# The last block's tail of a gated attention kernel: three groups' sums and half the projection taken out of it, transfers and store on two queues

## The chip, the cores and the metric

The kernel runs on one core of one Trainium2 chip. The time is the device time of one execution in microseconds (us), the median of several. One further execution was taken with the hardware profiler; the profile and the trace come from it. The engines are called PE (TensorE, matrix products; PEld is its weight load), DVE (VectorE), ACT (ScalarE), POOL (GpSimd) and SP (SyncE, which here only issues transfers). SP and ACT each have a queue on which they issue DMA transfers.

## The reference

The input x has the shape 4 x 2048 x 256, in float32. A layer norm gives xn. One branch is causal attention with 16 heads of 16 columns, rotary positions and an output projection; the other is a feed-forward net with ternary weights and a SiLU behind it, which gates the first:

```python
x = L0_attn_x
xn = _layernorm(x, axis=-1)
s = attention(xn)          # softmax(q k^T / 4, causal) v, then @ Wo.T + bo
g = _silu(ffn(xn))         # ternary W1, gelu, ternary W2
x = x + s * g
```

What matters here is the end of the attention: for each query the weighted sum of the values is divided by the sum of the softmax's exponentials, multiplied by Wo, has bo added, is multiplied by the gate and added to x.

## The kernel before, in words

The 8192 rows are worked off in 16 blocks (`NBLK`) of 512 queries (`NB`), four blocks (`NQ`) for each of the four sequences. A block's 16 heads go in four groups (`G`) of four heads. A loop over the 64 pairs of block and group (from line 1017) runs, for each group, the steps of `values`: scores (L771), exponentials (L778 on ACT), the causal mask on the diagonal (L782 on POOL) and the product with the values (L795), summed up in one PSUM bank `av`. Each head has 32 rows of `av`: 16 of the weighted values, one of the sum of exponentials. Beside them the loop hands out other work: the maxima of the next group (`maxima`, L685 to L745, with its reductions on DVE), the projections of a later block, its feed-forward net, and, one at each step, the entries of a list `deferred`. The order in which things are written is the order on each engine; nothing reorders them afterwards, so an instruction that waits holds up what stands behind it on its engine.

When a group is through, `end` (L820) runs in the first step of the following group, or behind the loop for the very last one. It copies `av` to `av_sb` (L824, ACT) and issues, head by head, two transfers on SP: `y` (L831), 16 rows of 512 values, to the rows of the head in the tile `ys[blk]`, and `w` (L836), the 512 sums laid out as 8 rows of 64 in the tile `ws[blk]`, so that a block's 16 heads fill 128 rows of 64. Head d of the block lies in half `kc` = d // 8 of `y`: two halves of 128 rows.

Behind a block's fourth group `end` puts the steps of `finish(blk)` (L847) on `deferred`:

- `loaded` (L853): x of the block is loaded again, 512 KB, on SP.
- `inverted` (L857, L858): DVE takes the reciprocal of the 128 x 64 sums, and SP writes them to DRAM (`rd`).
- `spread` (L866): SP reads them back in two transfers of 256 KB (`rw`), each head's row of 512 repeated for its 16 rows.
- `divided(kc)` (L876): DVE multiplies `y` by `rw`, one half at a time.
- `projected(dc)` (L886, L893): two products with Wo, one for each `kc`, summed up in a bank; in the profile each is two instructions. DVE adds bo and multiplies by the gate, which gives `s`.
- `added(t2)` (L909, L915): four transposes of `s` on PE, and DVE adds x. Behind the second of them SP stores the block's 512 KB (L924).

In all blocks but the last these steps lie beside the groups of the next block. In the last block nothing follows: behind the loop (L1071 to L1075) the last `end` and then the whole of `finish` run alone.

Of the kernel before, what the change touches and what calls it, by code (L numbers as in the profile page):

```python
# [9 lines left out]
F32 = mybir.dt.float32  # L10
# [4 lines left out]
ALU = mybir.AluOpType  # L15
# [4 lines left out]
P = 128  # L20
NB = 512
TT = NB // P
H = 16
HD = 16
HF = HD // 2
G = 4
GH = H // G
# [11 lines left out]
def attention_gated_by_ffn(  # L39
# [33 lines left out]
    nc = tc.nc  # L73
    B, T, D = x.shape
    FF = w1.shape[0]
    KC = D // P
    FC = FF // P
    NQ = T // NB
    NBLK = B * NQ
# [5 lines left out]
    out_blk = out.rearrange("b (n t p) d -> (b n) p t d", t=TT, p=P)  # L85
# [12 lines left out]
    def bank(name):  # L98
        i = free_banks.pop(0)
        taken.setdefault(name, []).append([i])  # L100
        return psum[:, i, :]
# [30 lines left out]
    woT = const.tile([P, KC, D], F32, name="woT")  # L132
# [619 lines left out]
    def values(blk, g):  # L752

        n = blk % NQ
        mT, q = mTs.pop((blk, g)), qst[blk, g]
        last = (n + 1) * TT - 1
        pending, exs = [], {}

        def scores(kb, j, q0):
            s2 = two_banks("s2")  # L760
            w = NB - q0

            at = NB - 2 * P if kb == last else 0
            if not at:
                exs[j] = pp.tile([P, 2, NB], F32, tag="e", name="e")
            e = exs[j][:, :, at : at + w]
            for part in range(2):
                for a in range(2):
                    rows = slice(a * ST, (a + 1) * ST)
                    k = kst[blk, g, kb // TT][rows, j, (kb % TT) * P : (kb % TT + 1) * P]  # L770
                    nc.tensor.matmul(  # L771
                        s2[:, a, :w],
                        (k, sels[j][rows, :])[part],
                        (q[rows, j, q0:], mT[rows, q0:])[part],
                        start=(part == 0),
                        stop=(part == 1),
                    )
            nc.scalar.activation(e, s2[:, :, :w], AF.Exp, scale=1.0 / math.sqrt(HD))  # L778
            release("s2")
            if kb >= n * TT:  # L780

                nc.gpsimd.affine_select(  # L782
                    out=e[:, :, :P],
                    in_=e[:, :, :P],
                    pattern=[[0, 2], [1, P]],
                    compare_op=ALU.is_ge,
                    fill=0.0,
                    base=0,
                    channel_multiplier=-1,
                )  # L790
            return e

        def times_v(kb, ex, q0):
            for h in range(GH):
                nc.tensor.matmul(  # L795
                    av[h * HP : (h + 1) * HP, q0:],
                    vst[blk, g, kb // TT][:, kb % TT, h * VE : h * VE + HP],
                    ex[h // 2][:, h % 2, : NB - q0],
                    start=(kb == 0),
                    stop=(kb == last),  # L800
                )
            if kb % TT == TT - 1:
                vst.pop((blk, g, kb // TT))
                loads.release("v")

        for kb in range(last + 1):
            q0 = max(kb - n * TT, 0) * P
            ex = [scores(kb, j, q0) for j in range(GH // 2)]
            if kb % TT == TT - 1:
                kst.pop((blk, g, kb // TT))  # L810
                loads.release("k")
            yield
            if kb < last:
                while pending:
                    times_v(*pending.pop())
            pending.append((kb, ex, q0))
            yield
        qst.pop((blk, g))

        def end():  # L820
            for chunk in pending:
                times_v(*chunk)
            av_sb = one.tile([P, NB], F32, tag="av_sb", name="av_sb")
            nc.scalar.copy(av_sb, av)  # L824
            if g == 0:
                ys[blk] = yp.tile([P, KC, NB], F32, tag="y", name="y")
                ws[blk] = small.tile([P, H * NB // P], F32, tag="w", name="w")

            for h in range(GH):
                d = (g * GH + h) * HD  # L830
                nc.sync.dma_start(  # L831
                    out=ys[blk][d % P : d % P + HD, d // P, :],
                    in_=av_sb[h * HP : h * HP + HD, :],
                )
                a = (g * GH + h) * P // H
                nc.sync.dma_start(  # L836
                    out=ws[blk][a : a + P // H, :],
                    in_=av_sb[h * HP + HD : h * HP + HD + 1, :].rearrange(
                        "o (a k) -> o a k", a=P // H
                    ),  # L840
                )
            if g == G - 1:
                deferred.extend(finish(blk))

        ends.append(end)

    def finish(blk):  # L847

        got = {}

        def loaded():
            got["x"] = one.tile([P, TT, D], F32, tag="xr", name="x_res")
            nc.sync.dma_start(out=got["x"], in_=x_blk[blk])  # L853

        def inverted():
            w = ws.pop(blk)
            nc.vector.reciprocal(w, w)  # L857
            nc.sync.dma_start(  # L858
                out=rd[blk].rearrange("h (a k) -> (h a) k", k=H * NB // P), in_=w
            )  # L860

        def spread():

            r = got["r"] = one.tile([P, KC, NB], F32, tag="rw", name="rw")
            for kc in range(KC):
                nc.sync.dma_start(  # L866
                    out=r[:, kc, :],
                    in_=rd[blk][kc * (P // HD) : (kc + 1) * (P // HD)]
                    .unsqueeze(1)
                    .to_broadcast([P // HD, HD, NB]),  # L870
                )

        def divided(kc):
            if kc == 0:
                got["yT"] = tp.tile([P, KC, NB], F32, tag="tT", name="yT")
            nc.vector.tensor_tensor(  # L876
                got["yT"][:, kc, :], ys[blk][:, kc, :], got["r"][:, kc, :], ALU.mult
            )

        def projected(dc):  # L880
            if dc == 0:
                ys.pop(blk)
                got["s"] = tp.tile([P, KC, NB], F32, tag="tT", name="s")
            po = bank("po")
            for kc in range(KC):
                nc.tensor.matmul(  # L886
                    po,
                    woT[:, kc, dc * P : (dc + 1) * P],
                    got["yT"][:, kc, :],
                    start=(kc == 0),  # L890
                    stop=(kc == KC - 1),
                )
            nc.vector.scalar_tensor_tensor(  # L893
                got["s"][:, dc, :],
                po,
                boc[:, dc : dc + 1],
                gs[blk][:, dc, :],
                ALU.add,
                ALU.mult,
            )  # L900
            release("po")

        def added(t2):
            x_sb, s = got["x"], got["s"]
            pt = bank("pt")
            for j in range(2):
                t = 2 * t2 + j
                for dc in range(KC):
                    nc.tensor.transpose(  # L909
                        pt[:, (2 * j + dc) * P : (2 * j + dc + 1) * P],  # L910
                        s[:, dc, t * P : (t + 1) * P],
                        ident,
                    )
            ts2 = slice(2 * t2, 2 * t2 + 2)
            nc.vector.tensor_tensor(  # L915
                x_sb[:, ts2, :],
                pt.rearrange("p (t d) -> p t d", t=2),
                x_sb[:, ts2, :],
                ALU.add,
            )  # L920
            release("pt")
            if t2 == TT // 2 - 1:
                gs.pop(blk)
                nc.sync.dma_start(out=out_blk[blk], in_=x_sb)  # L924

        if (blk + 1) % NQ == 0:

            steps = [None, loaded, None, None, inverted, None, spread, None, None]
            steps += [lambda: [divided(kc) for kc in range(KC)]]
        else:  # L930
            steps = [None, loaded, None, None, inverted, None, spread, None]
            steps += [lambda kc=kc: divided(kc) for kc in range(KC)]
        steps += [lambda dc=dc: projected(dc) for dc in range(KC)]
        steps += [None]
        steps += [lambda t2=t2: added(t2) for t2 in range(TT // 2)]
        return steps

# [1 line left out]

    deferred, ends = [], []

    class Paced:

# [10 lines left out]
        def rest(self):  # L956
            for _ in self.gen:
                pass
# [172 lines left out]
```

## Time and profile before

| | us |
|---|---|
| median of three runs (lowest, highest) | 2438.69 (2438.4, 2438.8) |
| the profiled execution, its own time | 2433.26 |
| its span, from the first to the last instruction | 2431.5 |
| PE busy in the span | 2303.4 |
| DVE, ACT, POOL busy | 1624.9, 1467.2, 893.9 |
| start of the last group's copy (L824) | 2404.04 |
| issue of the last store (L924) | 2427.67 |

The mean granted TensorE clock was 0.985 of full speed. Times inside the profile count from the start of the span. Between the span and the execution's own time lie 1.8 us. Where the text speaks of the landing of a transfer, it is the time from its issue to the last arrival at its semaphore, from the records of the single transfers in the trace. These are the main ones of the last block:

| transfer | size | issue | to landing, us |
|---|---|---|---|
| last `w` (L836) | 2 KB | 2409.40 | 1.71 |
| `rd` (L858) | 32 KB | 2411.97 | 2.35 |
| first `rw` (L866) | 256 KB | 2414.33 | 3.79 |
| second `rw` (L866) | 256 KB | 2415.00 | 4.69 |
| store (L924) | 512 KB | 2427.67 | 2.92 |

### The profile page before, as it was taken

The numbers are of one execution on the slowest core, as the hardware profiler recorded it, in microseconds if no ns is written. First come the engines' busy times: TensorE is split into PE (matmuls) and PEld (weight loads), VectorE is DVE, ScalarE is ACT, GpSimd is POOL, SyncE is SP. The second block draws the span as 40 slices with busy tenths as digits, with TensorE's granted clock in tenths as the row PEclk, the third lists the DMA queues.
The fourth block names the chain that finished last, engine by engine and source line by source line (L and its number), as shares of the span: only waits on it lengthen the run. The fifth ranks groups of instructions, "written<-read, shape, count | busy, mean of one in ns | idle before, by whom it ended". The sixth has DMA issues, their size and how long they took to land.

```text
span 2431.5 us, 43963 instructions
## 1 busy us (share of the span) xinstructions
PE 2303.4 (95%) x16852; PEld 1228.4 (51%) x16852; DVE 1624.9 (67%) x2923; ACT 1467.2 (60%) x1871; POOL 893.9 (37%) x1312
## 2 busy tenths in 40 slices
PE   6799999999999999999999999999999999999996
PEld 4454545545455455544545455454554545455442
DVE  8656677775556676696636668768663666777880
ACT  3454656656765565765766465565676646566664
POOL 2136343235443535315344542522625453531010
PEclk8899999999999999999999999999999999999998
DMA  7344334234253524224234443413524452432311
GB/s 222 110 134 152 98 118 154 65 103 134 79 167 103 180 86 158 76 89 148 63 125 124 149 140 111 151 55 89 169 61 136 125 189 77 132 120 72 86 35 32
DMA packets 247907, 280.59 MB, mean 115 GB/s; under 512 B 108816, under 2 KB 144016, under 8 KB 247696
## 3 DMA queue, kind: packets, MB, share of 16 engines
q1 hardware_dynamic: 244368, 272.54, 35.5%
q10 hardware_dynamic: 3328, 5.24, 0.6%
q8 instruction: 132, 2.16, 0.4%
q14 instruction: 79, 0.65, 0.1%
HBM read 181.08 MB, written 87.52 MB: 110 GB/s over the span
## 4 chain that ended last, share of the span: by engine, by line
PE 73%; DVE 10%; POOL 6%; ACT 6%; issue 3%; DMA 1%; SPq 0%; ACTq 0%; DVEq 0%; POOLq 0%
PE psum L771 19%; PE psum L795 19%; PE psum L685 14%; PE psum L581 5%; PE psum L494 4%; PE psum L562 4%; DVE mx L707 3%; DVE mx L711 3%; PE psum L697 3%; PE psum L520 2%; PE psum L886 2%; ACT e L778 2%; ACT mT L745 1%; POOL qklo L378 1%; ACT g L589 1%
## 5 line engine op out<-in xcount | busy, mean ns | idle before, releaser
L707 DVE TENSOR_REDUCE mx<-psum 128x1 f32<-128x512 f32 (+1 forms) x2048 | 1261.7, 667 | 504.5 <-PE psum L685 348.5
L778 ACT ACTIVATE e<-psum 128x1024 f32<-128x1024 f32 (+3 forms) x1280 | 1081.0, 894 | 646.9 <-PE psum L771 611.5
L685 PE MATMUL psum<-kst,qst 64*128 64x512 f32 (+3 forms) x2560 | 618.9, 423 | 18.8 <-ACT e L778 5.5
L795 PE MATMUL psum<-e,vg 128*32 128x512 f32 (+3 forms) x5120 | 595.0, 541 | 17.3 <-POOL e L782 17.1
L782 POOL TENSOR_SCALAR_AFFINE_SELECT e<-e 128x256 f32<-128x256 f32 x512 | 205.7, 411 | 1010.1 <-ACT e L778 980.4
L771 PE MATMUL psum<-qst,kst 64*128 64x512 f32 (+3 forms) x2560 | 553.5, 395 | 21.0 <-DVE mx L707 5.7
L685 PEld LDWEIGHTS psum<-kst,qst 64*128 64x128 f32 x2560 | 311.3, 185 | 449.8 <-DVE mx L707 284.5
L771 PE MATMUL psum<-mT,sel 64*128 64x512 f32 (+3 forms) x2560 | 515.8, 371 | 6.0 <-ACT mT L745 2.9
L771 PEld LDWEIGHTS psum<-qst,kst 64*128 64x128 f32 x2560 | 283.2, 186 | 171.9 <-ACT e L778 54.9
L771 PEld LDWEIGHTS psum<-mT,sel 64*128 64x128 f32 x2560 | 272.2, 186 | 43.3 <-ACT mT L745 23.2
L575 POOL TENSOR_TENSOR hl<-h,hh 128x512 fp32r<-128x512 f32 x128 | 165.3, 1298 | 155.6 <-ACT h L573 121.5
L795 PEld LDWEIGHTS psum<-e,vg 128*32 128x32 f32 x5120 | 110.0, 108 | 176.3 <-issue 123.1
L711 DVE TENSOR_REDUCE mx<-psum 128x3 f32<-128x384 f32 x256 | 130.3, 552 | 73.8 <-PE psum L697 73.8
L697 PE MATMUL psum<-parts 64*128 64x128 bf16 (+1 forms) x1536 | 151.3, 242 | 0.0
L573 ACT ACTIVATE hh<-psum,b1c 128x512 fp32r<-128x512 f32 x128 | 88.1, 688 | 85.4 <-PE psum L562 85.2
L494 PE MATMUL psum<-xf,wqkvT 128*128 128x512 f32 x256 | 127.8, 624 | 0.4 <-ACT xf L439 0.4
L562 PE MATMUL psum<-xh,w1T 128*128 128x512 f32 x256 | 107.8, 421 | 0.7 <-POOL xh L377 0.5
L581 PE MATMUL psum<-hh,w2T 128*128 128x512 f32 x256 | 107.7, 421 | 0.2 <-ACT w2T L348 0.2
L562 PE MATMUL psum<-xl,w1T 128*128 128x512 f32 x256 | 103.2, 403 | 1.1 <-POOL xl L378 1.1
L581 PE MATMUL psum<-hl,w2T 128*128 128x512 f32 x256 | 103.1, 403 | 0.8 <-POOL hl L575 0.2
L502 ACT ACTIVATE qk<-psum,bqk 128x512 f32<-128x512 f32 x64 | 43.9, 688 | 86.7 <-PE psum L494 85.8
L573 ACT ACTIVATE h<-psum,b1c 128x512 f32<-128x512 f32 x128 | 87.3, 682 | 0.0
(128 smaller groups left out, 1643.2 us busy)
## 6 DMA issues: line engine op xcount, KB each, us to landing
kst<-kd SPq DMA_DIRECT2D x160, 512.0 KB
qst<-qd SPq DMA_DIRECT2D x64, 512.0 KB
vg<-vd SPq DMA_DIRECT2D x160, 166.0 KB
qd<-qkhi SPq DMA_DIRECT2D x32, 512.0 KB
qd<-qklo SPq DMA_DIRECT2D x32, 512.0 KB
kd<-qkhi SPq DMA_DIRECT2D x30, 512.0 KB
kd<-qklo SPq DMA_DIRECT2D x30, 512.0 KB
vd<-v SPq DMA_DIRECT2D x16, 574.0 KB
```

Of the source, the lines that this page charges most:

```text
L494: nc.tensor.matmul(pq, wqkvT[:, kc, at : at + P], xf[:, kc, :], start=(kc == 0), stop=(kc == KC - 1),)
L562: nc.tensor.matmul(ph, w1T[:, kc, f * P : (f + 1) * P], x12[:, kc, :], start=(kc + i == 0), stop=(kc + i == KC),)
L573: nc.scalar.activation(to, ph, AF.Gelu, bias=b1c[:, f : f + 1])
L581: nc.tensor.matmul(pgs[dc], w2T[:, f - 2, dc * P : (dc + 1) * P], hx, start=(f - 2 + i == 0), stop=(f - 2 + i == FC),)
L685: nc.tensor.matmul(s1[:, at : at + wt], q[rows, j, t * P : (t + 1) * P], kst[blk, g, c][rows, j, :wt], start=(at == 0), stop=(c < n),)
L697: nc.tensor.matmul(s1[:, w - len(ts) * P : w], parts[rows, i, 0, :], parts[rows, i, 1 : 1 + len(ts), :], start=False, stop=(i == 1),)
L707: nc.vector.tensor_reduce(mx[:, 2 * j + a, at : at + 1], s1[:, :w], AX.X, ALU.max)
L711: nc.vector.tensor_reduce(mx[:, 2 * j + a, at : at + w // P], s1[:, :w].rearrange("p (b k) -> p b k", k=P), AX.X, ALU.max,)
L771: nc.tensor.matmul(s2[:, a, :w], (k, sels[j][rows, :])[part], (q[rows, j, q0:], mT[rows, q0:])[part], start=(part == 0), stop=(part == 1),)
L778: nc.scalar.activation(e, s2[:, :, :w], AF.Exp, scale=1.0 / math.sqrt(HD))
L782: nc.gpsimd.affine_select(out=e[:, :, :P], in_=e[:, :, :P], pattern=[[0, 2], [1, P]], compare_op=ALU.is_ge, fill=0.0, base=0, channel_mult ...
L795: nc.tensor.matmul(av[h * HP : (h + 1) * HP, q0:], vst[blk, g, kb // TT][:, kb % TT, h * VE : h * VE + HP], ex[h // 2][:, h % 2, : NB - q0 ...
```

## The change

It concerns the last block alone. `finish` returns for it a new list of steps, `in_parts()`, and the list is used in two pieces. Up to its `None` it is put on `deferred` when the third group's `end` runs, so it lies in the first seven steps of the fourth group: x is loaded; the sums of the first three groups, 96 rows of `w`, are inverted and written to `rd`; two `rw` transfers spread them (128 rows for the first half, 64 for the second); DVE divides those 128 and 64 rows. The rest runs behind the fourth group's `end`: the products of the first half with both halves of Wo, the reciprocal of the last 32 rows, their `rd`, one `rw` of 64 rows, the division of 64 rows, then for each `dc` the product of the second half and the gate, and `added`.

Behind the fourth group the four `y` transfers are issued on ACT's queue instead of SP's. The store goes out in two halves of 256 KB: the first behind the first addition on ACT, the second behind the second addition on SP.

In the order on each engine nothing else differs: PE has the four instructions of the first half's products directly behind the last L795, and SP has the four `w` behind the `rw` transfers of the first three groups.

```diff
             for h in range(GH):
                 d = (g * GH + h) * HD
-                nc.sync.dma_start(
+                queue = nc.scalar if tail and g == G - 1 else nc.sync
+                queue.dma_start(
                     out=ys[blk][d % P : d % P + HD, d // P, :],
...
-            if g == G - 1:
+            if tail and g >= G - 2:
+                if g == G - 2:
+                    last_steps.extend(finish(blk))
+                for _ in range(last_steps.index(None) if g == G - 2 else len(last_steps)):
+                    deferred.append(last_steps.pop(0))
+            elif g == G - 1:
                 deferred.extend(finish(blk))
...
-        def inverted():
-            w = ws.pop(blk)
+        def inverted(rows=slice(0, P)):
+            w = ws[blk][rows]
             nc.vector.reciprocal(w, w)
...
-        def spread():
+        def spread(*pieces):
...
+            for kc, lo, hi in pieces or [(kc, 0, P) for kc in range(KC)]:
+                heads = slice((kc * P + lo) // HD, (kc * P + hi) // HD)
                 nc.sync.dma_start(
-                    out=r[:, kc, :],
-                    in_=rd[blk][kc * (P // HD) : (kc + 1) * (P // HD)]
+                    out=got["r"][lo:hi, kc, :],
+                    in_=rd[blk][heads]
                     .unsqueeze(1)
-                    .to_broadcast([P // HD, HD, NB]),
+                    .to_broadcast([(hi - lo) // HD, HD, NB]),
                 )
...
+        def in_parts():
+            at = (G - 1) * GH * HD - P
+            heads = slice(0, (G - 1) * P // G)
+            steps = [loaded, lambda: inverted(heads)]
+            steps += [lambda: None, lambda: spread((0, 0, P), (1, 0, at))]
+            steps += [lambda: None, lambda: divided(0), lambda: divided(1, 0, at), None]
+
+            def first():
+                got["s"] = tp.tile([P, KC, NB], F32, tag="tT", name="s")
+                got["po"] = [bank("po") for dc in range(KC)]
+                for dc in range(KC):
+                    product(dc, 0)
+                inverted(slice(heads.stop, P))
+                spread((1, at, P))
+                divided(1, at, P)
+
+            def product(dc, kc):
+                nc.tensor.matmul(
+                    got["po"][dc],
+                    woT[:, kc, dc * P : (dc + 1) * P],
+                    got["yT"][:, kc, :],
+                    start=(kc == 0),
+                    stop=(kc == KC - 1),
+                )
+
+            def rest(dc):
+                product(dc, 1)
+                gated(dc, got["po"][dc])
+
+            steps += [first] + [lambda dc=dc: rest(dc) for dc in range(KC)]
+            return steps + [lambda t2=t2: added(t2) for t2 in range(TT // 2)]
...
             release("pt")
-            if t2 == TT // 2 - 1:
+            if blk == NBLK - 1:
+                queue = (nc.scalar, nc.sync)[t2]
+                queue.dma_start(out=out_blk[blk][:, ts2, :], in_=x_sb[:, ts2, :])
+            elif t2 == TT // 2 - 1:
                 gs.pop(blk)
                 nc.sync.dma_start(out=out_blk[blk], in_=x_sb)
 
+        if blk == NBLK - 1:
+            return in_parts()
```

`gated` is the old second part of `projected` (L893), made a function of its own.

More of the change, by code (lines that the diff above doesn't have):

```diff
@@ L827, in end @@
                 ws[blk] = small.tile([P, H * NB // P], F32, tag="w", name="w")
+            tail = blk == NBLK - 1
             for h in range(GH):
                 d = (g * GH + h) * HD
-                nc.sync.dma_start(
+                queue = nc.scalar if tail and g == G - 1 else nc.sync
+                queue.dma_start(
                     out=ys[blk][d % P : d % P + HD, d // P, :],
@@ L853, in loaded @@
             nc.sync.dma_start(out=got["x"], in_=x_blk[blk])
-        def inverted():
-            w = ws.pop(blk)
+        def inverted(rows=slice(0, P)):
+            w = ws[blk][rows]
             nc.vector.reciprocal(w, w)
             nc.sync.dma_start(
-                out=rd[blk].rearrange("h (a k) -> (h a) k", k=H * NB // P), in_=w
+                out=rd[blk].rearrange("h (a k) -> (h a) k", k=H * NB // P)[rows], in_=w
             )
-        def spread():
-            r = got["r"] = one.tile([P, KC, NB], F32, tag="rw", name="rw")
-            for kc in range(KC):
+        def spread(*pieces):
+            if "r" not in got:
+                got["r"] = one.tile([P, KC, NB], F32, tag="rw", name="rw")
+            for kc, lo, hi in pieces or [(kc, 0, P) for kc in range(KC)]:
+                heads = slice((kc * P + lo) // HD, (kc * P + hi) // HD)
@@ L866, in spread, with divided @@
                 nc.sync.dma_start(
-                    out=r[:, kc, :],
-                    in_=rd[blk][kc * (P // HD) : (kc + 1) * (P // HD)]
+                    out=got["r"][lo:hi, kc, :],
+                    in_=rd[blk][heads]
                     .unsqueeze(1)
-                    .to_broadcast([P // HD, HD, NB]),
+                    .to_broadcast([(hi - lo) // HD, HD, NB]),
                 )
-        def divided(kc):
-            if kc == 0:
+        def divided(kc, lo=0, hi=P):
+            if "yT" not in got:
@@ L875, in divided @@
                 got["yT"] = tp.tile([P, KC, NB], F32, tag="tT", name="yT")
             nc.vector.tensor_tensor(
-                got["yT"][:, kc, :], ys[blk][:, kc, :], got["r"][:, kc, :], ALU.mult
-            )
+                got["yT"][lo:hi, kc, :],
+                ys[blk][lo:hi, kc, :],
+                got["r"][lo:hi, kc, :],
+                ALU.mult,
+            )
+        def in_parts():
[25 more added lines that the diff above has]
+            return steps + [lambda t2=t2: added(t2) for t2 in range(TT // 2)]
@@ L892, in projected, with gated @@
                 )
+            gated(dc, po)
+        def gated(dc, po):
             nc.vector.scalar_tensor_tensor(
@@ L936, in finish @@
         return steps
-    deferred, ends = [], []
+    deferred, ends, last_steps = [], [], []
     class Paced:
```

## The prediction

> **What bounds the kernel now.** I read the page first, then the stretches of the tail, then the chain of waits there. On the page TensorE is busy 95% of the span, and only its first and last slices are not full:
>
> ```profile
> PE 2303.4 (95%) x16852; PEld 1228.4 (51%) x16852; DVE 1624.9 (67%) x2923; ACT 1467.2 (60%) x1871; POOL 893.9 (37%) x1312
> PE   6799999999999999999999999999999999999996
> PEclk8899999999999999999999999999999999999998
> ```
>
> All edits lie in the last block, and the order of instructions on each engine is the same up to there, so only the tail matters. The table by stretches (columns: length, then busy time of PE, its weight loads, DVE, ACT and POOL, granted clock, DMA share, GB/s) shows it:
>
> ```profile
> 2370.00:2404.00 34.00, 33.45 (x274) 13.72 (x272) 0.00 (x0) 29.44 (x34) 3.51 (x9) 1.00 0.02 5
> 2404.00:2411.40 7.40, 0.00 (x0) 0.00 (x0) 0.01 (x1) 0.58 (x1) 0.00 (x0) 0.66 0.10 22
> 2411.40:2418.90 7.50, 0.01 (x1) 0.01 (x1) 1.23 (x2) 0.00 (x0) 0.00 (x0) 0.50 0.44 141
> 2418.90:2423.50 4.60, 4.60 (x6) 1.88 (x7) 1.41 (x2) 0.00 (x0) 0.00 (x0) 0.50 0.00 1
> ```
>
> In the last group's 34 us DVE has nothing to do and the DMA engines are 2% busy; then TensorE stands still for 14.9 us and works at half clock when it starts again. The chain of waits says what fills that time (start, length, what):
>
> ```profile
> 2404.04 0.59 ACT av_sb L824
> ...
> 2404.65 0.54 SPq L831
> ...
> 2408.82 0.53 SPq L831
> ...
> 2409.40 1.71 DMA w<-av_sb
> ...
> 2411.39 0.56 DVE w L857
> ...
> 2411.97 2.35 DMA rd<-w
> ...
> 2414.33 3.79 DMA rw<-rd
> ...
> 2418.15 0.70 DVE yT L876
> ...
> 2418.89 5.98 PE psum L886 x8
> ...
> 2424.97 0.76 DVE s L893
> ```
>
> Copy, eight issues on SP one behind the other, three transfers in series, then division, projection, turning and store: 27.5 us from 2404.04 to the span's end at 2431.53.
>
> **The change, part by part.** I follow the new chain on the clock of this execution.
>
> *Work put beside the last group.* Load of x, reciprocal of 96 rows, one rd, two rw, two divisions. The w rows of the third group land at 2378.21 + 1.71 = 2379.9; then 0.55 (reciprocal), about 2.3 (rd behind the 512 KB of x), 0.7 and 4.7 (second rw), 0.69 (division) put the last of it at about 2389. The cover is DVE's zero in the first stretch and the 2% of DMA; the first user is the product behind the group at 2404, 15 us later. POOL's masks there begin at 2398.0, after it. On SP these issues stand ahead of the last four w only, which can't start before the copy at 2404.6. Without this cover nothing else would be gained either. Cost: 0. The first half of the projection does not run inside the group: in TensorE's order its four instructions stand behind the last L795. They take 4 x 0.43 = 1.7 us at full clock, to 2405.8, while transfers run: 0, and it shortens what comes later.
>
> *Four y issues to ACT, x and four y off SP.* w0 goes out at 2404.65 in y0's place. Starts of a w and of the issue behind it are 0.69 apart (2405.23, 2405.93), so w3 starts at 2404.65 + 3 x 0.69 = 2406.72 instead of 2409.40: **-2.68**. ACT has no other work left. No row has both queues issuing here; at the kernel's start ACT's four loads took 0.51 to 0.71 us each beside SP's issues, so up to 0.2 a piece may be lost (0.8), and nothing can be won. I take 0.69, the row of the same instruction. y3 lands about 2404.65 + 3 x 0.6 + 1.9 = 2408.4, far ahead of its use.
>
> *Inverse sums of one group.* w3 lands 1.71 after its issue, at 2408.43. DVE started 0.27 behind the landing, through its waits on eight semaphores; with four I take 0.20 (**-0.07**). The reciprocal stays 0.55: the length along a row is still 64. rd took 2.35 here with the 512 KB of x in flight beside it. The 16 rd transfers of the trace took 1.44 to 1.50 where nothing ran beside them, 1.9 to 2.1 with other traffic. Now x is long in place: 1.45 (**-0.90**, with 2.0 only -0.35). So rw3 is issued at 2408.63 + 0.55 + 0.03 + 1.45 + 0.02 = 2410.68.
>
> *One rw of 64 partitions.* No such transfer is in the trace. Above stand the first rw of each block (128 partitions), 3.50 to 4.11 us, 3.79 here; below, a y of 32 KB, 1.9. While the two rw run (2415.75 to 2418.90) the DMA share is 0.50, so half of the 16 engines carry them, at 16 rows of 2 KB each for a transfer of eight heads. If four heads use four engines, the length stays; if the engines stay eight, each moves 8 rows of some 0.09 us less, about 2.9. I take 3.6, near the full one's row but without a second transfer behind it. The Trainium skill says in "DMA: Bandwidth & Descriptors", section "Why a DMA increments its semaphore by 16 and not by 1", that a transfer runs on the largest number up to 16 that divides the slowest dimensions of both patterns. Eight heads and 128 partitions give 8, which the share 0.50 agrees with; four heads and 64 partitions would give 4, and so the full 3.8. It lands at 2414.28.
>
> *Division and second half.* Division 0.69, then 0.05 to TensorE: 2414.30 to 2415.05, where the old kernel began its second-half product at 2420.76. From rw's issue to that product it was 6.43 and is now 3.6 + 0.02 + 0.69 + 0.06 = 4.37: **-2.06**. TensorE has then been idle for 9 us, so the clock is 0.5 as at 2418.9, where it stayed so for 4.6 us. Cold pairs of L886 are 0.85 apart and the first took 1.01. s0 starts at 2415.05 + 1.01 + 1.06 + 0.11 = 2417.23 and s1 at 2418.94: 3.89 from the product's start, against 4.21 (2420.76 to 2424.97): **-0.32**.
>
> *Turning.* The eight transposes ran at clock 1.0 in 0.11 each. Now the clock would rise only about 2419.7 (4.6 behind 2415.05), and with pauses between. From s1's start to the end of the last addition it was 2.68. If they stay cold at twice the spacing, the first addition waits for three cold ones and the second for four more: 0.75 + 0.05 + 0.06 + 2 x 0.21 + 0.42 + 0.04 to the first, 0.86 and 0.69 behind it, together 3.3: **+0.6**. If warm, 0. I take cold.
>
> *Two halves of the store.* The first goes out on ACT, some 0.9 us ahead of the second on SP. The whole took 2.92 at a DMA share of 0.91, some 1.4 of it moving; a 256 KB store to DRAM alone (cs, L275) took 2.0. I take 2.2 for the second half: **-0.7**, with 0 if they only queue and -0.9 by the cs row. The Trainium skill speaks against this part: "DMA: Bandwidth & Descriptors", section "Rules for kernel authors", says of two transfers to disjoint partition halves "Don't bother — they serialize"; by that the term is 0 and the sum one of 5.4 us. These halves are of columns, but share engines as well; the share of 0.91 shows that one store fills them.
>
> *Sum:* -2.68 - 0.07 - 0.90 - 2.06 - 0.32 + 0.6 - 0.7 = -6.1, rounded to **-6.0 us**. The span goes from 2431.5 to 2425.5, the execution's own 2433.26 to 2427.3. The median of the runs shown is 2438.69, 5.4 above this execution; the tail is the same work there, so I take the same difference: **2432.7 us**.
>
> Bounds: every term at its poor end gives -1.9 - 0 - 0.35 - 1.5 - 0.3 + 0.6 - 0 = -3.5, at its good end (rw 2.9, warm transposes, store 2.0) -2.7 - 0.1 - 0.9 - 2.8 - 0.3 + 0 - 0.9 = -7.7; rw at y's 1.9 would give -8.7.
>
> **Rivals.**
> - *The small rw is quick, and the rest goes well.* For: 64 rows are half the bytes. Against: only eight engines carried the whole. rw at 2.8 gives -6.9: 2431.8 us. Chance 0.20.
> - *Two queues act as one.* Issues of ACT and SP alternate as on one queue and the halves of the store queue behind each other. For: one set of engines. Against: the DMA share is 0.10 in 2404 to 2411, so it is SP's issue time of 0.54 to 0.65 that fills it, and ACT issued at the start in no more than 0.71 beside SP. The terms 2.68 and 0.7 go: -2.7, 2436.0 us, within 0.2%. Chance 0.14.
> - *Slower: y from ACT's queue comes late.* The last division needs all four y. They have slack from 2408.4 to 2414.3, and the sign turns when y3 lands behind 2414.3 + 6.0 = 2420.3, 15.7 us behind the copy; at 2423 the time is 2441.4. For: ACT's queue had been unused since the first 100 us. Against: its own loads at the kernel's start, in the fullest traffic of the trace, landed in 4.4 to 6.9. Chance 0.03.
> - *It doesn't do what it says:* the first half of the projection stands behind the group, not beside it; that is in the sum already and changes nothing.
>
> **How the numbers follow.** Forecast 0.63, quick rw 0.20, one queue 0.14, late y 0.03. About 0.2% (4.9 us) is what a measurement of this kernel tells from no change, so "faster" means below 2433.8. Of the forecast's own 0.63 I put 0.05 above that (poor rd and store together): faster 0.78, same 0.19, slower 0.03. The range takes in the bounds -3.5 and -7.7 and half a microsecond of spread below: 2430.5 to 2435.2; it leaves out the one-queue case and the late y, 0.17.
>
> **What would show it.** In the chain of waits after: only w issues on SP's line, w3 at about 2406.7; rd about 1.5; rw about 3.6 (2.9 means eight engines); one division; L886's successor with four instructions on the chain at clock 0.5; the last store issued at about 2422.2 and landing 2.2 later. The forecast is wrong if w issues are spaced by over 0.9, if the chain passes through y or the store of ACT, or if anything before 2404 has moved by over 1 us.

## The result, and the profile after

| | before | after |
|---|---|---|
| median of 10 runs, us (lowest, highest) | 2437.24 (2433.17, 2439.42) | 2430.93 (2427.38, 2434.89) |
| the profiled execution, its own time | 2433.26 | 2429.44 |
| its span | 2431.5 | 2427.7 |
| start of the last group's copy (L824) | 2404.04 | 2405.84 |
| from there to the end of the span, "the tail" | 27.49 | 21.88 |

The ratio of the runs is 0.9977, with a 95% interval of 0.9969 to 0.9985: 0.23% faster, between 0.15% and 0.31%. In microseconds that is 5.6 (3.7 to 7.6) of 2437.24; the medians differ by 6.3. The forecast was 6.0 less, at 2432.7. The tail is 5.61 shorter. The difference of the spans, 3.8, is less because in the profiled execution after the last copy began 1.8 later. That is not the work put beside the last group: from the third group's copy to the last one it is 30.91 us in both kernels, so that work cost nothing, as the prediction said. The 1.8 is already there at the third group's copy (2373.13 before, 2374.92 after), where nothing is changed yet; the last section shows where it arises.

The chain of waits of the kernel after, from the copy on (start, length, what):

```profile
2405.84 0.59 ACT av_sb L824
...
2406.45 0.68 SPq L838
...
2407.17 0.71 SPq L838
...
2407.93 0.62 SPq L838
...
2408.59 2.02 DMA w<-av_sb
...
2410.72 0.56 DVE w L865
...
2411.30 1.36 DMA rd<-w
...
2412.68 3.67 DMA rw<-rd
...
2416.43 0.70 DVE yT L886
...
2417.17 3.80 PE psum L912 x4
...
2421.06 0.76 DVE s L943
...
2421.86 1.77 PE psum L959 x7
```

SP's issues are all of L838, the sums `w`; those of `y` are on ACT and no longer in the chain. One rw and one division are left, and four instructions of the projection instead of eight. What has become longer stands at two places: the last w (2.02 against 1.71) and the transposes, 1.77 for seven. In the old chain three of them took 0.56, and then the additions on DVE set the pace:

```profile
2425.77 0.56 PE psum L909 x3
```

The stretches of the kernel after (length, busy time of PE, its weight loads, DVE, ACT and POOL, granted clock, DMA share, GB/s):

```profile
2405.80:2412.60 6.80, 1.90 (x4) 0.59 (x4) 0.55 (x1) 0.59 (x1) 0.00 (x0) 1.00 0.11 22
2412.60:2417.20 4.60, 0.03 (x1) 0.03 (x1) 0.69 (x1) 0.00 (x0) 0.00 (x0) 0.50 0.09 28
2417.20:2421.90 4.70, 4.00 (x6) 1.36 (x6) 1.50 (x2) 0.00 (x0) 0.00 (x0) 0.50 0.00 0
2421.90:2424.40 2.50, 1.72 (x7) 1.31 (x7) 1.37 (x2) 0.00 (x0) 0.00 (x0) 0.50 0.00 0
```

The four instructions of the first half run at full clock beside the transfers (1.90 us of PE in the first stretch). All that TensorE does behind the pause runs at half clock, the transposes too, which in the old kernel had the full clock back:

```profile
2423.50:2427.70 4.20, 2.45 (x12) 1.18 (x10) 2.07 (x4) 0.00 (x0) 0.00 (x0) 1.00 0.00 0
```

### The profile page after: what moved, and what is told of

Same layout as the page of the kernel before. It is cut to its first block, busy times and chain, and to the rows that moved or that the text cites. A ratio compares the mean times of both kernels' runs of the same rounds, so it can differ in the third digit from the quotient of the medians.

```text
span 2427.7 us, 43974 instructions
## 1 busy us (share of the span) xinstructions
PE 2303.4 (95%) x16852; PEld 1227.2 (51%) x16852; DVE 1626.6 (67%) x2925; ACT 1468.1 (60%) x1871; POOL 895.5 (37%) x1312
## 3 DMA queue, kind: packets, MB, share of 16 engines
q8 instruction: 132, 2.16, 0.4%
## 4 chain that ended last, share of the span: by engine, by line
PE 72%; DVE 10%; ACT 6%; POOL 6%; issue 3%; DMA 2%; SPq 1%; ACTq 0%; DVEq 0%; POOLq 0%
PE psum L771 19%; PE psum L795 19%; PE psum L685 14%; PE psum L581 5%; PE psum L562 4%; PE psum L494 4%; DVE mx L707 3%; DVE mx L711 3%; PE psum L697 3%; PE psum L520 2%; ACT e L778 2%; PE psum L933 2%; ACT mT L745 1%; POOL qklo L378 1%; ACT g L589 1%
## 5 line engine op out<-in xcount | busy, mean ns | idle before, releaser
L795 PE MATMUL psum<-e,vg 128*32 128x512 f32 (+3 forms) x5120 | 596.2, 542 | 17.6 <-POOL e L782 17.4
L771 PEld LDWEIGHTS psum<-mT,sel 64*128 64x128 f32 x2560 | 271.4, 186 | 43.8 <-ACT mT L745 23.4
L795 PEld LDWEIGHTS psum<-e,vg 128*32 128x32 f32 x5120 | 109.9, 108 | 177.3 <-issue 124.8
```

The lines of the kernel that those rows point to most:

```text
L771: nc.tensor.matmul(s2[:, a, :w], (k, sels[j][rows, :])[part], (q[rows, j, q0:], mT[rows, q0:])[part], start=(part == 0), stop=(part == 1),)
L795: nc.tensor.matmul(av[h * HP : (h + 1) * HP, q0:], vst[blk, g, kb // TT][:, kb % TT, h * VE : h * VE + HP], ex[h // 2][:, h % 2, : NB - q0 ...
```

## The experiments

Each kernel is the changed one with one edit, and one profiled execution. The tail is counted from the start of the last copy, so that it doesn't depend on the work ahead of it. Where "the clock rose in time" is said, the transposes ran at full clock: they and their additions then take 0.68 less, and the second half of the store 0.17 more, since it follows the first closer. That makes a tail about 0.5 shorter, and with the same four instructions of the projection it happened in some executions and not in others. The records suggest that it depends on where the boundaries of the clock's stretches fall: in "one store", "rw by head" and "rw of eight heads" the clock fell 5.13 to 5.27 behind the copy and rose 15.4 to 15.5 behind it, in time; in the changed kernel, "y on SP" and "x late" it fell 5.71 to 6.87 behind the copy and didn't rise again. From the store's landing to the end of the span it is 0.9 to 1.1 in all of them.

| kernel | tail, us | last w lands behind the copy | rd | last rw | first of the last products to second gate step | that step to the end of the additions | store behind its last issue |
|---|---|---|---|---|---|---|---|
| before | 27.49 | 7.07 | 2.35 | 4.69 | 6.08 (both halves) | 2.68 | 2.92 |
| after | 21.88 | 4.77 | 1.36 | 3.67 | 3.89 | 3.36 | 2.17 |
| y on SP | 23.75 | 6.83 | 1.36 | 3.48 | 3.89 | 3.35 | 2.16 |
| one store | 21.71 | 4.76 | 1.36 | 3.44 | 3.89 | 2.68 | 2.93 |
| x late | 22.75 | 4.78 | 2.22 | 3.73 | 3.88 | 3.36 | 2.16 |
| projection behind | 23.23 | 4.76 | 1.36 | 3.82 | 5.60 | 2.68 | 2.35 |
| sums late | 23.37 | 5.18 | 1.45 | 4.63 | 5.50 (both halves) | 2.68 | 2.35 |
| rw by head | 20.95 | 4.76 | 1.36 | 3.21 (four) | 3.89 | 2.68 | 2.33 |
| rw of eight heads | 21.45 | 4.77 | 1.35 | 3.75 | 3.89 | 2.68 | 2.35 |
| warm | 19.19 | 4.63 | 1.35 | 3.37 | 2.09 | 2.75 | 2.33 |
| warm, again | 19.68 | 4.80 | 1.36 | 3.67 | 2.09 | 2.75 | 2.34 |
| turned | 11.85 | none | none | none | 2.02 | 2.74 | 2.34 |

**y on SP.** My theory was that SP's issue time fills the stretch behind the copy; the rival, that the two queues work as one.

```diff
-                queue = nc.scalar if tail and g == G - 1 else nc.sync
+                queue = nc.sync
```

> The tail is counted from the start of the last copy (L824) to the end of the span: 27.49 us before, 21.88 us after the change. Here the four y of the last group go back to SP, the rest stays changed. Theory (SP's issue time is what fills this stretch): the last w is issued about 5.1 to 5.4 us behind the copy's start instead of 2.75, and lands in 1.71 again instead of 2.02; tail 23.9 to 24.3. Rival (the two queues share what makes the transfers, so the second queue saved nothing and the gain came from elsewhere): tail 21.9.

The last w was issued 5.13 behind the copy's start and landed 1.70 later; the reciprocal began at 6.96 instead of 4.89. The tail was 23.75, a little under the expected range, since its rw took 3.48 instead of 3.67. The second queue is worth 2.07 us; the rival falls. But it has a price: beside ACT's transfers the w take 2.02 to 2.22 instead of 1.69 to 1.75.

**One store.**

```diff
-            if blk == NBLK - 1:
-                queue = (nc.scalar, nc.sync)[t2]
-                queue.dma_start(out=out_blk[blk][:, ts2, :], in_=x_sb[:, ts2, :])
-            elif t2 == TT // 2 - 1:
+            if t2 == TT // 2 - 1:
```

> The store is one transfer of 512 KB on SP behind the second addition, as before; the rest stays changed. Theory (the first half is under way while the second addition runs): the store lands 2.9 us behind its issue instead of 2.17, tail 22.6. Rival (two halves only queue behind each other on the same engines): tail 21.9.

The tail, 21.71, agrees with neither: the clock rose in time (-0.68) and rw was 0.23 shorter. The term itself is plain in its row: 2.93 behind the issue, against 2.17. With the two other differences taken out the tail would be 22.6. The halves are worth 0.75 at half clock; at full clock, where the additions follow closer, the second half takes 2.33 to 2.35, and 0.6 is left. The Trainium skill's "Don't bother — they serialize" ("DMA: Bandwidth & Descriptors", section "Rules for kernel authors") is said of halves of the partitions, and does not settle this case: here the first half is issued 0.9 us ahead, while DVE still adds for the second, so it is time that is won, not bandwidth.

**x late.**

```diff
-            steps = [loaded, lambda: inverted(heads)]
+            steps = [lambda: None, lambda: inverted(heads)]
...
+                loaded()
                 inverted(slice(heads.stop, P))
```

> The load of x (512 KB) is moved back into the tail, on SP between the last w and rd, as in the kernel before; the rest stays changed. Theory (rd is short in the changed kernel because x no longer moves beside it): rd takes 2.2 to 2.4 us instead of 1.36, tail 22.8. Rival (rd is short because it has 32 rows instead of 128): rd stays at 1.4, tail 21.9.

The chain of waits of this kernel has rd with x in flight beside it:

```profile
2410.87 2.22 DMA rd<-w
```

Tail 22.75 with the rest as after: the traffic of x costs rd 0.86 us. The number of rows counts for little: 128 rows took 2.35 in the kernel before beside x, and 1.45 in "sums late" without it, each some 0.1 more than 32 rows. Here the first theory holds in both numbers.

**Projection behind.** The edit moves the first half's products into the two steps of the second.

```diff
-                for dc in range(KC):
-                    product(dc, 0)
                 inverted(slice(heads.stop, P))
...
             def rest(dc):
+                product(dc, 0)
                 product(dc, 1)
```

> The first half's products with Wo are put back behind the last division, so all eight instructions of the projection lie in the path; the rest stays changed. Theory (they ran at half clock in the path): the second gate step starts about 6.1 us behind the first product instead of 3.9; the transposes behind it get the full clock back if the clock rises in time (2.7 us instead of 3.36 to the end of the second addition): tail 23.4, and 25.3 if it doesn't rise. Rival (TensorE's part of this change is worth nothing, since what counts are the transfers): tail 21.9 to 22.2.

The edit did less than the expectation says: the first half's product for `dc` = 0 waits for nothing and still ran beside the copy; only that for `dc` = 1, two instructions, came into the path. The chain has six instead of four:

```profile
2420.58 5.50 PE psum L910 x6
```

1.71 more to the second gate step is twice the 0.853 between two instructions at half clock. The clock rose in time, and rw was 0.15 longer; that the tail of 23.23 is near the expected 23.4 is no test of that number, as the edit was half as large. The rival falls all the same: work of TensorE in the path is paid in full, at half clock.

**Sums late.** The other large part: reciprocal, both rw, both divisions and both halves of the projection in the tail again, only x beside the last group.

```diff
-            steps = [loaded, lambda: inverted(heads)]
-            steps += [lambda: None, lambda: spread((0, 0, P), (1, 0, at))]
-            steps += [lambda: None, lambda: divided(0), lambda: divided(1, 0, at), None]
+            steps = [loaded, None]
...
+                inverted()
+                spread()
+                divided(0)
+                divided(1)
                 for dc in range(KC):
                     product(dc, 0)
-                inverted(slice(heads.stop, P))
-                spread((1, at, P))
-                divided(1, at, P)
```

> Only the load of x stays beside the last group; reciprocal, rd, both rw and both divisions of the whole block and both halves of the projection stand in the tail again, with y on ACT and the store in two halves as changed. Tail after the change: 21.88 us. Theory (the early sums save the second rw behind the first and the first half's products at half clock): the first division starts about 10.7 us behind the copy's start, the first product 0.75 later, the second gate step about 6.1 behind that (3.9 in the changed kernel), and the transposes run at full clock if it rises in time: tail 23.3 to 23.7, and 25 at half clock. Rival (the second rw lands while TensorE works on the first half, so the early sums are worth nothing): tail 21.9.

Tail 23.37, first division at 11.06, first product at 11.81, second gate step 5.50 behind it. The rival falls: 1.49 us more in all. But 0.47 of it is that the reciprocal began later, because the w landed later in this execution, for which I have no reason. The clock rose while the eight products ran:

```profile
2425.00:2428.50 3.50, 3.43 (x4) 1.52 (x5) 0.71 (x2) 0.00 (x0) 0.00 (x0) 0.50 0.02 6
2428.50:2432.60 4.10, 3.28 (x13) 1.46 (x11) 2.13 (x4) 0.00 (x0) 0.00 (x0) 1.00 0.00 0
```

To the second gate step it is 17.31 here and 15.22 in the changed kernel. So the early sums take 2.1 us out of the path, 1.6 without the late w. The tail differs by 0.5 less, since here the clock rose for the transposes; as it did so in three kernels with the short work too, that is not shown to be due to the longer work.

The 1.6 is TensorE's alone (5.50 against 3.89). The rival is right in its premise: the second rw landed 12.72 behind the copy and its division was done at 13.54, while TensorE was at the first half's four instructions until 15.32, so the second rw cost nothing. What the early sums win is that the first half's products can run beside the copy and the transfers.

**rw by head and rw of eight heads.** What sets the length of the one rw that is left?

```diff
-                spread((1, at, P))
+                for i, lo in enumerate(range(at, P, HD)):
+                    h = (P + lo) // HD
+                    (nc.sync, nc.scalar)[i % 2].dma_start(
+                        out=got["r"][lo : lo + HD, 1, :],
+                        in_=rd[blk][h : h + 1].unsqueeze(1).to_broadcast([1, HD, NB]),
+                    )
```

> The last rw is cut into four transfers of one head (16 rows) each, two on SP and two on ACT. Tail after the change: 21.88 us. Theory (the one rw of four heads runs on four DMA engines with 16 rows each, and so is as long as a full one of eight heads on eight): each small one runs on 16 engines and lands about 2.0 behind its issue like a y, the second on each queue 0.6 later: 2.6 to 2.9 us instead of 3.67 from the first issue to the last landing, tail 20.8 to 21.1. Rival (its length is the fixed cost of a read from DRAM, whatever the engines): 3.0 plus 0.6 for the second issue, tail 21.8 to 22.5.

```diff
-                spread((1, at, P))
+                spread((1, 0, P))
```

> The last rw reads all eight heads of the second half (128 rows, 256 KB) instead of four (64 rows, 128 KB); the division stays at 64 rows. The four heads read again are the same values. Theory (engines are as many as heads, up to eight, each with 16 rows): twice the bytes in the same 3.7 us, tail 21.9. Rival (the length goes with the bytes): 0.7 us more, tail 22.6.

The eight heads took 3.75, within the 3.37 to 3.82 that four heads take in the other kernels: twice the bytes at no cost. In the records the semaphore of the changed kernel's rw has four arrivals behind the issue's own, here it has eight, and the DMA share while the rows move is twice as high. First the kernel after, then the one with eight heads:

```profile
2414.10:2416.00 1.90, 0.00 (x0) 0.00 (x0) 0.00 (x0) 0.00 (x0) 0.00 (x0) 0.50 0.19 68
```

```profile
2416.00:2417.80 1.80, 0.00 (x0) 0.00 (x0) 0.00 (x0) 0.00 (x0) 0.00 (x0) 0.50 0.41 146
```

Cut by heads, each small rw has 16 arrivals and lands 2.04 to 2.63 behind its issue. From the first issue to the last landing it is 3.21, 0.3 more than the theory allowed: that four at once on two queues slow each other, as the w did beside the y, is likely but was not tried apart. DVE then started 0.32 behind the landing, through waits on seven semaphores, where it was 0.08. The first product came 11.10 behind the copy instead of 11.33: the gain is 0.23, and the rest of the shorter tail is the clock that rose in time and 0.2 at the very end. The idea of the engines agrees with the arrivals and the lengths; it is worth next to nothing in this form.

**Warm.** Ten products that nobody reads keep TensorE busy through the transfers.

```diff
+                idle_bank = bank("pd")
+                for _ in range(10):
+                    nc.tensor.matmul(
+                        idle_bank, woT[:, 0, :P], got["yT"][:, 0, :], start=True, stop=True
+                    )
                 inverted(slice(heads.stop, P))
```

> Ten more products of the first half, into a bank that nothing reads, stand behind the first products, so that TensorE is busy until about 1 us before the last half's products. They are extra work without a use. Theory (the second half and the transposes are slow because the granted clock is 0.5 after the pause): the clock stays 1.0, the second gate step starts 2.1 us behind the first of the last products instead of 3.9, and its start to the end of the second addition takes 2.7 instead of 3.36: tail 19.5. Rival (these steps are bound by waits and fixed latencies): tail 21.9; if the extra products run into the last ones, 22 to 23.

The tail was 19.19, and the second gate step came 2.09 behind the first of the last products, as expected:

```profile
2414.10:2425.00 10.90, 10.49 (x24) 4.40 (x24) 1.24 (x2) 0.59 (x1) 0.00 (x0) 1.00 0.11 27
2425.00:2427.00 2.00, 1.98 (x4) 0.68 (x4) 0.74 (x1) 0.00 (x0) 0.00 (x0) 1.00 0.00 0
2427.00:2429.90 2.90, 1.30 (x9) 0.89 (x8) 2.05 (x4) 0.00 (x0) 0.00 (x0) 1.00 0.00 0
```

The clock stays at 1.00, and 1.80 + 0.61 us go from the two steps: that is what the pause cost behind it in the changed kernel's execution. The rival falls. Yet the execution's time was 2435.05, because its last copy began at 2414.14. So it was run once more.

> The kernel with ten extra products, once more and unchanged, since in its first profile the last copy began 8.3 us later than in the changed kernel, though nothing before it differs. Theory (the work before the tail varies from execution to execution by the stretches in which the granted clock is 0.5 there): the copy begins between 2404 and 2410, the tail stays at 19.2. Rival (the longer tail of instructions slows the work before it): the copy begins at 2414 again.

The tail was 19.68 (its rw 3.67 instead of 3.37), the copy at 2411.44 and the time 2432.85: later than I allowed, so the bound of 2410 was wrong. That the extra products are to blame is not borne out either: "sums late" has none, and its copy began at 2413.27. These single times say nothing of the edit; whether it pays in the run's time was not measured with more runs.

**Turned.** If the tail is a series of transfers, a path without them should win what is left. The last group's y, w, rd and rw are dropped; the same quotient is formed by way of transposes. `last_av` keeps the copied sums, and `z` is a tile of zeros into which the last group's columns are written.

```diff
-            for h in range(GH):
+            for h in range(0 if tail and g == G - 1 else GH):
...
-                for dc in range(KC):
-                    product(dc, 0)
-                inverted(slice(heads.stop, P))
-                spread((1, at, P))
-                divided(1, at, P)
+                z = pp.tile([P, 2, NB], F32, tag="e", name="z")[:, 0, :]
+                z = z.rearrange("p (t c) -> p t c", c=P)
+                nc.gpsimd.memset(z, 0.0)
+                product(0, 0)
+                pt = bank("pt")
+                for t in range(TT):
+                    cols = slice(t * P, (t + 1) * P)
+                    nc.tensor.transpose(pt[:, cols], last_av[0][:, cols], ident)
+                product(1, 0)
+                pt_h = pt.rearrange("p (t h e) -> p t h e", h=GH, e=HP)
+                inv = small.tile([P, TT, GH], F32, tag="m", name="inv")
+                nc.vector.reciprocal(inv, pt_h[:, :, :, HD])
+                nc.vector.tensor_tensor(
+                    z[:, :, at:].rearrange("p t (h e) -> p t h e", e=HD),
+                    pt_h[:, :, :, :HD],
+                    inv.unsqueeze(3).to_broadcast([P, TT, GH, HD]),
+                    ALU.mult,
+                )
+                release("pt")
+                pt = bank("pt")
+                for t in range(TT):
+                    nc.tensor.transpose(pt[:, t * P : (t + 1) * P], z[:, t, :], ident)
+                nc.scalar.copy(got["yT"][at:, 1, :], pt[at:, :])
+                release("pt")
```

> The last group's y, w, rd and rw are gone: four transposes bring the copied sums to one row per query, DVE inverts 4 x 4 sums per row and multiplies, four transposes bring the result back, ACT copies it to the rows of the second half. Same result by another way. Theory (what is left of the tail is the series of transfers, so a path without transfers takes them all away): from the copy's start to the last half's first product about 3.3 us instead of 11.3, clock 1.0 all the way, tail 11 to 12, time about 10 us below the changed kernel and 16 below the one before (ratio 0.9935). Rival (each hop between engines costs as much as a short transfer): tail 15 to 17.

Its chain of waits from the transposes of the copied sums to the second gate step's additions:

```profile
2410.89 0.45 PE psum L914 x4
...
2411.43 0.27 DVE inv L918
...
2411.80 0.43 DVE z L919
...
2412.28 0.67 PE psum L928 x4
...
2412.97 0.59 ACT yT L929
...
2413.60 2.00 PE psum L933 x4
```

From the copy to the last half's products it is 3.72 us instead of 11.33, the pause is gone, and with it the half clock. Tail 11.85. Six runs gave a median of 2421.58 us (2419.41 to 2427.81), with a ratio of 0.9939 to the kernel before (0.9922 to 0.9955): 0.61% faster, between 0.45% and 0.78%. The theory's 0.9935 lies inside. It was not timed against the changed kernel directly, but its interval lies wholly below that kernel's (0.9969 to 0.9985).

## Why the prediction was right, step by step

| step of the sum | forecast | measured |
|---|---|---|
| four y issues off SP, last w issued earlier | -2.68 | -2.61 |
| the last w's landing (1.71 to 2.02) | 0 | +0.31 |
| DVE's waits before the reciprocal | -0.07 | -0.15 |
| rd without x beside it | -0.90 | -0.99 |
| from rw's issue to the product (6.43 to 4.49) | -2.06 | -1.94 |
| product to the second gate step | -0.32 | -0.32 |
| transposes and additions at half clock | +0.6 | +0.68 |
| store in two halves | -0.7 | -0.75 |
| behind the store's landing (0.94 to 1.11) | 0 | +0.17 |
| sum | -6.1, rounded to -6.0 | -5.60 |

The mechanism was right in the main, and no step is off by over 0.31 us. That one is the term that the prediction left at nothing: it bounded the issues of two queues that work at once, but not the landings, and those are what got longer. "y on SP" shows it by its opposite: alone on the queue the w land in 1.70 again. The other miss, 0.17 at the very end, was not followed up. For the issues on ACT the prediction took 0.51 to 0.71 us as their bound beside SP's; a little later in that trace, at 34 to 36 us, ACT's issues (L483) took up to 1.27. The four y took 0.60 to 0.63, so it did no harm.

The term from rw's issue to the product needs a word on what it holds. In the kernel before, the second rw landed 15.65 behind the copy and its division was done at 16.47, but TensorE was at the first half until 16.72 anyway. So the second rw was not on the path; 1.87 of the 1.94 are the first half's product that stood ahead (two instructions at half clock), and only the rest is the shorter rw and its neighbours.

The term of the clock was partly luck. The prediction let the clock rise 4.6 us behind the first product and so took the transposes as cold. In the profiled execution they were cold, but in three of the six kernels with these same four instructions the clock rose 4.0 to 4.4 us behind the first product and they ran warm, so the +0.6 is not a fixed cost.

One of the signs of being wrong, "if anything before 2404 has moved by over 1 us", did come true: the last copy began 1.80 later. That speaks against the sign, not against the mechanism: in two executions of the one kernel "warm" the copy began 2.70 apart.

For rw the prediction chose 3.6 by the row of the full one, and named the four engines as the reason why half the bytes need not be faster; 3.67, four engines and the run with eight heads bear that out, and the rival with the quick rw (2.8) falls. The rival of one queue falls with "y on SP". y came early as forecast: all four landed 4.6 us behind the copy, and the last division waited for rw until 10.5 behind it. That the first half of the projection would run behind the group, not in it, is what the order and the profile show.

The size: 5.6 in the tail against 6.0. The absolute time, 2430.93 against 2432.7, is lower than forecast for another reason: the ten runs of the kernel before have a median of 2437.24, 1.45 under the three that were shown. It lies only 0.4 above the lower end of the range, so with runs that spread from 2427 to 2435 it is partly luck that the absolute time fell inside. By the ratio the gain is 0.23%, barely over the 0.2% that the chances used, and its interval reaches below that bound.

## What to carry to other kernels

At the end of a kernel, where nothing is left to put beside it, count the chain hop by hop: the issue time of each queue, each transfer from its issue to its landing, and the clock at which TensorE comes back from the pause. Work whose inputs are ready goes beside the last full stretch, and big loads away from small transfers in the path; but a hop through DRAM that only changes a layout is worth more if it is replaced, as eight transposes did here (3.7 us for 11.3). Measure such a change in the stretch itself, since single times vary by more than it is worth.

## What the runs showed of the hardware that was not expected

Up to the last group all these kernels are the same, that group takes 30.89 to 30.92 us in each of them, and still the last copy began between 2404.04 and 2414.14 us. Compared with the kernel before, the shift at 210 us lies between -1.7 and 1.6 us. From there on it changes mostly in steps at stretches in which the granted clock is 0.5 in one of the two, near 720 to 820, 1364 to 1411 and 1898 to 1997 us; smaller steps, up to 0.9 us near 1336 and 1922, go with no such stretch. Each such stretch is 3.41 us long (one 6.83), and most steps are 1 to 2 us; in "warm" the stretch of 6.83 at 724 goes with a step of 6.7, and in its repetition one of 3.41 at 1898 with 3.6. The Trainium skill says in "TensorE: Matmul & The Clock Gate", section "What's actually happening", that the clock is set by free-running windows of 3413 ns; the records agree: those that end before the profile does are of 3.41 us or multiples of it (6.83, 10.24, 13.65, 17.07). If so, where a window falls decides whether a short pause costs clock. That the steps come from these stretches is read from their places; no experiment took a pause away there.

The number of heads that an rw reads, four or eight, set the number of arrivals at its semaphore; its length was 3.37 to 3.82 us for four heads' 128 KB and 3.75 for eight heads' 256 KB.
